# Layer 3 of a four-layer convolution network: the steps that make the next quarter's band matrices stand behind every second turn of patch products, four or five at a time

## The chip, the core and the metric

The kernel runs on one core of one Trainium2 chip, as one program. The metric is the device time of an execution in microseconds; the time before is the median of three runs.

## The reference

The input `x` is 16 images of 64 x 64 pixels with 256 channels, float32. Four layers follow each other, each of the form x = x + layer(groupnorm(x)): layer 0 is a linear attention over the pixels, layer 1 a channel and spatial gate with a state-space scan, layer 2 a 3 x 3 involution, layer 3 a 7 x 7 involution. Only layer 3 is touched here:

```python
r = jnp.einsum('bhwc,cd->bhwd', x, w_reduce)                 # 256 -> 64 channels
r = jax.nn.relu((r - mean) * (gamma / jnp.sqrt(var + BN_EPS)) + beta)
kgen = jnp.einsum('bhwd,de->bhwe', r, w_span) + b_span       # 49 weights for each of 16 groups
kgen = kgen.reshape(B, H, W, G, K * K)
...
out = jnp.einsum('bhwgk,bhwkgc->bhwgc', kgen, patches)       # each pixel: its own 7 x 7 kernel
```

Each pixel makes its own 7 x 7 kernel for each of 16 groups of 16 channels, and applies it to its neighbourhood.

## The kernel before

The kernel is written with a tile framework: the Python code issues instructions engine by engine, pools hand out buffers, and a scheduler decides in which order each engine's instructions stand and puts in the semaphore waits. The order in the code is the main guide of that scheduler, not the last word: it may take an instruction ahead of others of the same engine.

In layer 3 an image is cut into tiles of 3 x 8 output pixels (`TR, TC = 3, 8`): 22 rows of 8 tiles, 176 tiles, and the 16 groups into four quarters of four groups. A tile's input is a patch of 9 x 14 = 126 pixels. The products are matrix products over those 126 pixels:

- `reduced` (line 1425, tile `pr`) makes the 64 channels of `r`, and ACT writes them into `rt` (line 1432). One image has 11 such steps, issued during the image before, one every third turn (`features`); each loads a tile `c3` two turns ahead.
- `matrices(i, quarter)` is a generator of 24 steps per quarter. Each step makes the 126 x 24 band matrix columns of four output pixels for all 176 tiles: four matmuls (line 1458) write a PSUM tile `pk` of two banks, and then either four ACT activations (line 1468) or one VectorE add (line 1473) write it, with the bias, into the SBUF tile `wm`. Steps 1, 3, 6, 8 and 11 of each twelve go to ACT, the others to VectorE. [...]
- `involution7` (line 1524) is one turn of patch products: 32 matmuls, each of 126 rows by 32 columns, multiply the patches `xw` with the matrices `wm` into the PSUM tile `pa`. ACT (line 1536) and VectorE (line 1537) pick the group with a mask and write `ex`; GpSimd (line 1544) adds the residual `rx`. `pa` and `pr` share a PSUM pool `sm` of two buffers.

[...]

The main loop goes over 704 turns: 16 images, four quarters, 11 turns. SP issues all DMAs: the patches four turns ahead (two loads of 256 KB per turn, six `xw` buffers), the residual two turns ahead, the stores of `ex` three turns behind. The table `STEPS` says how many steps of the next quarter's matrices are issued behind each turn:

```python
for n, (i, quarter, t) in enumerate(turns):
    ...
    if t == 0:
        making = iter(())
        if n + NTT < len(turns):
            making = matrices(*turns[n + NTT][:2])
    ...
    involution7(i, quarter, t, wms[i, quarter], msk, pats.pop(0), ex[:, t % 2], rx[:, t % 2])
    ...
    for _ in range(STEPS[t]):
        next(making, None)
    if n in features:
        tp, k = features[n]
        reduced(k, tp, cs.pop((tp, k)))
    if t == NTT - 1:
        next(making, None)
```

The last line runs once more behind turn 10 (`NTT` is 11). With the table before, all 24 steps are issued by then, and it only ends the generator.

Of the kernel before, what the change touches and what calls it, by code (L numbers as in the profile page):

```python
# [36 lines left out]
def network(ctx: ExitStack, tc: tile.TileContext, a: dict, out: bass.AP):  # L37
# [767 lines left out]
    def centred_strips(i, u, xc, cen, mean):  # L805

        nc.gpsimd.tensor_tensor(
            cen.rearrange("p q t c -> p t q c"),
            xc.rearrange("p t (q c) -> p t q c", q=4),
            mean.rearrange("p (q c) -> p q c", q=4).unsqueeze(1).broadcast_to([P, 4, 4, 64]),  # L810
            ALU.subtract,
        )
        parts = []
        copies = [(u + 3, 0)] + [(u - 5, 1)] * (u >= TC - 3) + [(u + TC + 3, -1)] * (u < 3)
        for w, dt in copies:
            for th in range(2):
                t0, t1 = max(0, th * 4 + dt), min(NTC, th * 4 + 4 + dt)
                s0 = t0 - th * 4 - dt
                parts.append((
                    strips[i, :, 3 : 3 + HW, w, t0:t1, :].rearrange("q r t c -> r q (t c)"),  # L820
                    cen[th:P:2, :, s0 : s0 + t1 - t0, :].rearrange("p q t c -> p q (t c)"),
                ))
        return parts
# [540 lines left out]
    with ExitStack() as st:  # L1364
# [183 lines left out]


        turns = [(i, quarter, t) for i in range(NI) for quarter in range(4) for t in range(NTT)]  # L1550
        STEPS = (3, 2, 2, 3, 2, 3, 2, 2, 3, 2, 0)
        wms, cs, strip_stores = {}, {}, []
        features = {
            4 * NTT * i + 3 * k + 1: (2 * k, i + 1) for i in range(NI - 1) for k in range(NTT)
# [13 lines left out]
        for n, (i, quarter, t) in enumerate(turns):  # L1568
# [40 lines left out]
            if n % gap == 2 and n // gap < NCH:  # L1609
                cen = wk.tile([P, 4, 4, 64], F32, tag="xw", name="cen", bufs=6)  # L1610
                strip_stores.extend(centred_strips(NI - 1, n // gap, xc, cen, mean))
            for _ in range(STEPS[t]):
                next(making, None)
# [140 lines left out]
```

## Time and profile before

| | |
|---|---|
| median of 3 runs | 7944.51 us (7941.79 to 7947.63) |
| the profiled execution | 7971.0 us, span 7969.2 us |
| granted TensorE clock, mean over the span | 0.948 of full speed |
| busy share of the span | PE 86%, PEld 64%, DVE 71%, ACT 62%, POOL 38% |
| layer 3's main loop | 5682.9 to 7963.1 us of the span |
| in layer 3 (5690 to 7960 us) | PE busy 1966 us, ACT 1256, DVE 1047, POOL 452; DMA share 0.83 at 255 GB/s; clock 0.97 |

In the profile PE is TensorE's matmul, PEld its weight load, DVE VectorE, ACT ScalarE, POOL GpSimd and SP the engine that issues the DMAs. A row of the order of time has the start in us, the duration in us, the engine, the line, what is written and read, the shapes, how many instructions are merged in it, and in brackets the idle time before it and what ended it. A row of the waits has who waited for whom, the total in us, the number of times and the longest. A row of the chain has start, duration and what. A share of busy time is a mean over stages with different limits, so the stage is read by itself.

### The profile page before, as it was taken

How to read it: one execution, taken by the hardware profiler on the slowest of the kernel's cores; microseconds unless marked ns; L12 is line 12 of the kernel's file. 1: busy time of each engine (PE TensorE's matmuls, PEld its weight loads, DVE VectorE, ACT ScalarE, POOL GpSimd, SP SyncE). 2: the span in 40 equal slices, each digit the busy share in tenths (PEclk: the TensorE clock that was granted, in tenths of full speed). 3: DMA queues.
4: the chain of work that ended last, by engine and by line, in shares of the span. 5: the costliest groups of instructions: out<-in, count | busy, mean ns of one | idle time of the engine just before them, and what ended most of it. 6: DMA issues, size and time to landing. Idle time of an engine off the chain costs nothing.

```text
span 7969.2 us, 213876 instructions
## 1 busy us (share of the span) xinstructions
PE 6865.4 (86%) x88812; PEld 5137.4 (64%) x88812; DVE 5671.4 (71%) x6527; ACT 4934.1 (62%) x11456; POOL 3053.4 (38%) x2171
## 2 busy tenths in 40 slices
PE   7888888888888977689989999999788888888887
PEld 4666666666666664156666666666577777777776
DVE  6777777777777765879999999999444444444444
ACT  3555555555555554978787777776455555555554
POOL 1222222222222221168888888888222221111112
PEclk9999999999999986899999999999899999999999
DMA  7644444444443333967888888876688888888887
GB/s 216 196 149 133 138 137 133 135 135 135 134 137 112 117 103 103 327 209 264 285 282 286 270 287 275 288 265 224 209 259 260 258 255 261 256 253 258 248 257 236
DMA packets 1075308, 1689.89 MB, mean 212 GB/s; under 512 B 136273, under 2 KB 680354, under 8 KB 1073186
## 3 DMA queue, kind: packets, MB, share of 16 engines
q1 hardware_dynamic: 1074338, 1676.21, 65.4%
q8 instruction: 700, 11.47, 0.6%
q14 instruction: 270, 2.21, 0.1%
HBM read 1228.85 MB, written 469.76 MB: 213 GB/s over the span
## 4 chain that ended last, share of the span: by engine, by line
PE 46%; DVE 23%; issue 12%; ACT 8%; DMA 7%; POOL 3%; SPq 1%; DVEq 0%; POOLq 0%; ACTq 0%
PE pk L1458 13%; DVE pd L1185 9%; PE pa L1524 8%; PE pkv L270 5%; PE py L412 5%; DMA xn<-in_x 2%; PE pq L258 2%; PE pr L1425 2%; DVE x L1357 2%; PE pctx L336 2%; PE px L1097 1%; DVE mq L371 1%; ACT sq L421 1%; DVE z L1008 1%; DVE mq L378 1%
## 5 line engine op out<-in xcount | busy, mean ns | idle before, releaser
L1185 DVE TENSOR_TENSOR pd<-xs,pw 128x4608 f32<-128x4608 f32 x256 | 1256.0, 4947 | 5.5 <-POOL x L1199 5.3
L1458 PE MATMUL pk<-rt,span 64*128 64x176 f32 x12288 | 1183.6, 329 | 61.2 <-issue 55.0
L1468 ACT ACTIVATE wm<-pk,spanb 128x176 f32<-128x176 f32 x2560 | 845.8, 425 | 574.3 <-PE pk L1458 572.5
L1544 POOL TENSOR_TENSOR ex<-ex,rx 128x192 f32<-128x192 f32 (+2 forms) x768 | 436.7, 570 | 1826.5 <-DVE ex L1537 1329.4
L1198 POOL TENSOR_TENSOR pd<-pd 128x2048 f32<-128x2048 f32 (+2 forms) x384 | 1072.2, 2792 | 88.5 <-DVE pd L1185 68.4
L1458 PEld LDWEIGHTS pk<-rt,span 64*128 64x128 f32 x12288 | 973.2, 192 | 139.0 <-issue 81.3
L1537 DVE SCALAR_TENSOR_TENSOR ex<-pa,msk,ex 128x192 f32<-128x192 f32 x704 | 294.2, 418 | 1019.2 <-ACT ex L1536 951.9
L270 PE MATMUL pkv<-wq,xn 128*128 128x256 f32 x4096 | 979.3, 385 | 3.6 <-ACT va L279 2.0
L1524 PE MATMUL pa<-wm,xw 126*32 126x48 f32 x45056 | 751.1, 214 | 213.8 <-issue 201.0
L1473 DVE TENSOR_TENSOR wm<-pk,spanb 128x704 f32<-128x704 f32 x896 | 794.0, 888 | 192.0 <-PE pk L1458 188.8
L270 PEld LDWEIGHTS pkv<-wq,xn 128*128 128x128 f32 x4096 | 782.1, 194 | 229.3 <-issue 116.4
L366 POOL TENSOR_TENSOR qa<-qa,mq 128x1024 f32<-128x1024 f32 x256 | 501.5, 1980 | 1027.3 <-DVE mq L371 514.2
L1524 PEld LDWEIGHTS pa<-wm,xw 126*32 126x32 f32 x45056 | 620.8, 111 | 396.1 <-issue 352.0
L1147 PE MATMUL pt<-ident,pad 128*128 128x128 f32 x4608 | 604.6, 280 | 146.0 <-ACT xs L1151 122.7
L1147 PEld LDWEIGHTS pt<-ident,pad 128*128 128x128 f32 x4608 | 505.3, 142 | 294.1 <-ACT xs L1151 145.9
L1357 DVE TENSOR_REDUCE x<-pd 128x512 f32<-128x4608 f32 x128 | 634.0, 4953 | 4.4
L412 PE MATMUL py<-wo,o 128*128 128x256 f32 x2048 | 542.5, 422 | 64.8 <-ACT va L279 59.7
L1151 ACT COPY xs<-pt 128x512 f32<-128x512 f32 x1152 | 584.4, 597 | 17.5 <-PE pt L1147 17.4
L258 PE MATMUL pq<-xn,wq 128*128 128x512 f32 x1024 | 539.7, 644 | 34.1 <-ACT xn L133 21.6
L412 PEld LDWEIGHTS py<-wo,o 128*128 128x128 f32 x2048 | 496.2, 310 | 110.2 <-ACT va L279 76.9
L1536 ACT ACTIVATE ex<-pa,msk 128x192 f32<-128x192 f32 x704 | 299.7, 426 | 389.6 <-PE pa L1524 179.7
L1097 PE MATMUL px<-x2p,wis 128*128 128x512 f32 x1024 | 477.5, 610 | 46.1 <-ACT xs L1151 36.9
(243 smaller groups left out, 11780.3 us busy)
## 6 DMA issues: line engine op xcount, KB each, us to landing
xw<-strips SPq DMA_DIRECT2D x1408, 256.0 KB
xn<-in_x SPq DMA_DIRECT2D x256, 512.0 KB
x_d<-x SPq DMA_DIRECT2D x256, 512.0 KB
strips<-cen SPq DMA_DIRECT2D x352, 256.0 KB
xin<-in_x SPq DMA_DIRECT2D x128, 512.0 KB
x<-in_x SPq DMA_DIRECT2D x128, 512.0 KB
xm<-x_d SPq DMA_DIRECT2D x128, 512.0 KB
x2p<-x_d SPq DMA_DIRECT2D x128, 512.0 KB
```

Source lines behind the costliest of these rows:

```text
L258: nc.tensor.matmul(pq, lhsT=wq[:, h, f0 : f0 + P], rhs=xn[:, h], start=(h == 0), stop=(h == 1),)
L270: nc.tensor.matmul(pkv[:, q], lhsT=xn[:, h, q * P : (q + 1) * P], rhs=wq[:, h, f0 + P : f0 + 384], start=(h == 0), stop=(h == 1),)
L412: nc.tensor.matmul(py[:, q, :], lhsT=om[i, hf][:, :, ch * 4 + q], rhs=wo[:, hf, :], start=(hf == 0), stop=(hf == 1),)
L1147: nc.tensor.transpose(pt[:, k, h * P : (h + 1) * P], lines[:, h, rc * 4 + e + k, 2 * j : 2 * j + P], ident,)
L1151: nc.scalar.copy(xs[:, e : e + 2, j, :], pt)
L1185: nc.vector.tensor_tensor(pd.rearrange("p r (g f) k -> p r g f k", f=16), run, pw.rearrange("p r (g k) -> p r g k", k=9).unsqueeze(3).broa ...
L1198: nc.gpsimd.tensor_tensor(pd[..., 0:n], pd[..., 0:n], pd[..., n : 2 * n], ALU.add)
L1357: nc.vector.tensor_reduce(x3[:, :, P:C], pd1, AX.X, ALU.add)
L1458: nc.tensor.matmul(pkv[:, b, m], lhsT=span[half, first + gg, s0 : s0 + P], rhs=rto[half, o // 4 * 2 + m, :], start=True, stop=True,)
L1468: nc.scalar.activation(dst[:, m // 2, m % 2], pkv[:, m // 2, m % 2], AF.Identity, bias=spanb[:, g0 + m : g0 + m + 1],)
L1473: nc.vector.tensor_tensor(dst, pkv, spanb[:, g0 : g0 + 4].rearrange("p (b m) -> p b m", b=2).unsqueeze(3).broadcast_to([P, 2, 2, NTL]), AL ...
L1524: nc.tensor.matmul(pav[p0 : p0 + 32, :, tj * TC : (tj + 1) * TC].rearrange("c g (w v) -> c g w v", v=2), lhsT=xw[0:TILE_IN, k, tj, 32 * q ...
```

## The change

One line of the table changes. Counted over a quarter, 24 steps behind turns 0 to 9 become 23 behind turns 1, 3, 5, 7 and 9; the call behind turn 10 then issues the 24th.

```diff
         turns = [(i, quarter, t) for i in range(NI) for quarter in range(4) for t in range(NTT)]
-        STEPS = (3, 2, 2, 3, 2, 3, 2, 2, 3, 2, 0)
+        STEPS = (0, 5, 0, 4, 0, 5, 0, 4, 0, 5, 0)
         wms, cs, strip_stores = {}, {}, []
```

## The prediction

> **What bounds the kernel now.** I read three views of layer 3, the only stage that the diff touches (its first patch product starts at 5682.9 us and its last at 7963.1 us: 2280 us, 704 turns of 3.24 us, 64 quarters of 35.6 us). First the chain of work that ended last, in order of time, for a stretch of that stage:
>
> ```profile
> 7003.57 1.99 PE pk L1458 x24
> 7005.56 0.91 PE pa L1524 x57
> 7006.47 1.77 PE pk L1458 x16
> 7008.24 0.90 PE pa L1524 x58
> 7009.14 1.39 PE pk L1458 x16
> 7010.54 0.83 PE pr L1425 x8
> 7011.37 0.53 PE pa L1524 x30
> 7011.90 1.54 issue
> ```
>
> Everything on it is PE, or "issue": PE waited for nothing that the profile shows. ACT, VectorE, GpSimd and DMA do not appear. Over the whole stage the chain is PE and 11.4% issue, with some 6% of DMA and DMA issuing. Second, the waits of the stage:
>
> ```profile
> PE pa L1524 <- issue: 200.7, 197, 3.2
> PE pk L1458 <- issue: 55.0, 60, 2.4
> PEld pa L1524 <- DMA xw<-strips: 16.6, 46, 1.9
> PEld pa L1524 <- DVE wm L1473: 9.9, 30, 1.6
> PEld pa L1524 <- ACT wm L1468: 3.5, 15, 0.6
> ```
>
> The work that matters for this change, PE waiting until ACT or VectorE has emptied a PSUM buffer, costs some 15 us today. The idle time of "issue" is 256 us. Third, what this issue is: PE alone in order of time,
>
> ```profile
> 7013.44 0.58 PE L1524 MATMUL pa<-wm,xw 126*32 126x48 f32 x31 [1.54 <-issue]
> 7013.95 2.06 PE L1458 MATMUL pk<-rt,span 64*128 64x176 f32 x24
> 7015.94 0.96 PE L1524 MATMUL pa<-wm,xw 126*32 126x48 f32 x64
> 7016.83 1.01 PE L1458 MATMUL pk<-rt,span 64*128 64x176 f32 x9
> 7018.46 0.86 PE L1458 MATMUL pk<-rt,span 64*128 64x176 f32 x7 [0.62 <-issue]
> ```
>
> From one stall to the next PE ran 31 + 24 + 64 + 9 = 128 matmuls, each with its weight load: 256 instructions. The stall falls in the middle of runs, so it is no dependence. And the page's queue table has
>
> ```profile
> q8 instruction: 700, 11.47, 0.6%
> ```
>
> that is 700 transfers of 16.4 KB, and 2 x 88812 PE instructions with the 1622 of its sequencer make 179,246 = 700 x 256. So PE gets its program in blocks of 256 instructions and stands still when the next block is late. Counting the trace's records by blocks: 459 blocks in the stage, 4.96 us each on average; the q8 transfer for the next block starts 2.3 us (median) after a late block has begun (1.4 to 3.5), and PE goes on 2.44 us after it started. So a block hardly takes less than about 4.75 us, whatever is in it, and 280 of 458 begin late (over 0.35 us after the block before). PE's own work in a block, from the rows without stalls, is 4.1 us. The stage is bound by PE work and by instruction blocks in turn: each block costs the larger of the two.
>
> [...]
>
> **The change part by part.** It issues the same 24 steps per quarter, each of 4 matmuls in the program (8 weight loads and 8 matmul records) and one VectorE add or four ACT activations, no DMA. Before, 2 or 3 stand behind each of ten turns. After, five or four stand behind turns 1, 3, 5, 7, 9, and the 24th comes from the closing call behind turn 10. GpSimd's order is the same; on SP the same DMAs stand in a slightly different order (the loads of c3 and the stores of out shift by a turn at most), and I cost that at nothing: SP issues for 1960 of 2270 us and PE waits 25 us for xw in all; if that cover goes, the price is in the third rival.
>
> (a) Fewer changes of matmul form on PE. A run of 24 costs 1.99 us and one of 16 1.39 us, so 8 weight loads cost 0.60 us and entering a run 0.19 us; a turn's 64 products take 0.90 us up to the next run, of which 64 x 0.012 us (distance of weight loads inside the run) explains 0.77. Each avoided change there and back thus saves 0.19 + 0.13 = 0.32 us; by the distances between records (pk to pa 0.387 against 0.07 inside, pa to pk 0.185 against 0.012) it is 0.49 us. One might expect ten changes to become six per quarter, but the scheduler puts single pk matmuls ahead of or between the products: in the instruction order the returns to pa fall from 693 to 547. 146 x 0.32 to 0.49 = 47 to 72 us; I take -60, between the two rows.
>
> (b) New waits for PSUM buffers. pk has three buffers. With runs of 2 or 3 steps the fourth step never stands close behind the first. Now it does. From the ACT and VectorE rows: four activations take 1.33 us, an add 0.89 us, and the addition of the last turn's ex (0.42 us each on ACT and VectorE) stands ahead. Counting from the start of the run (pk at 7003.50, its first add 7004.41, its first activations 7005.07): the add of step 1 ends at 1.8 us, the activations of step 2 at 2.9 us; without a wait steps 4 and 5 would start at 1.8 and 2.4 us. Which steps ACT empties is fixed (1, 3, 6, 8, 11 of each 12). Run by run: in [add act add act add] the fifth step waits 0.5 us for step 2's activations; [add act add act] waits for nothing; in [add add act add act] the fifth waits 0.2 us for the second add; [add act add add] waits for nothing; in [act add act add add] the fourth waits 0.44 us for the activations of the first (0.9 to 2.24 us after the start). Together 1.14 us per quarter, 63 quarters: 72 us. The 24th step is emptied by ACT and stands right ahead of the next quarter's first turn, whose second product reads it: 0.2 us to the first activation and 1.33 us for the four, less 0.55 us of pk matmuls that the order slips in: 1.0 to 1.5 us, 63 to 95 us in all. Sum 135 to 167 us; bounds 0 (a wait cannot be negative; all of it may fall in time in which PE would wait for instructions) and 200 (the split runs delay further steps); I take 150. Behind such a wait on PE stand the products of the next turns and, every third turn, the matmuls of pr; ACT's and VectorE's ex, GpSimd's addition and the stores wait in turn, all with room (ACT is busy 1256 of 2270 us, VectorE 1047, GpSimd 452).
>
> (c) 138 more waiting instructions in PE's stream (685 for 547 in the stage), 0.05 us each by their rows: 7 us.
>
> Raw sum on PE: -60 + 150 + 7 = +97 us, between -65 and +160.
>
> (d) The blocks. Two turns of products back to back are 256 instructions, one block, in 1.8 us of PE work. I laid both orders out in blocks of 256, added up the durations above in each, and took 4.75 us wherever a block has less. Without any waits of (b): before 2232 us (measured 2280; the rest is chiefly what PE waited for DMA), after 2249: +17 although PE's work fell by 64, since blocks with under 2.5 us of work go from 5 to 55. With waits where they fall: blocks above 4.75 us go from 80 to 141, and the sum rises by 69 us; with 4.5 us for 4.75 it is 82, with 5.1 us 54. So the shortest block time hides about a third of (b). A further part goes because PE asks for the next block earlier when it has instructions in hand: blocks that had 0.7 to 1.2 us to spare asked 1.4 us after their start, not 2.3. I subtract a fifth for that: **+55 us**.
>
> The profiled execution took 7971.0 us (span 7969.2), 26.5 us over the median of 7944.5. So I expect a profile of about 8026 us and a median of 7944.5 + 55, about 8000 us.
>
> **Rivals.** Slower by far more: 55 blocks are used up in 2 us, the pair of turns needs two xw tiles at once, and SP (86% busy) has no room to catch up. The wait for xw then joins the sum: +69, and about 1 us per quarter, 64 us: about +135, 8080 us. For it: xw waits exist already. Against it: loads run four turns ahead, 13 us. It decides once the waits for xw, 25 us now, pass 90.
>
> No change: block loading alone sets the pace, 460 blocks for 459, the waits of (b) fall wholly inside late blocks. 0 to +15 us, 7945 to 7960. For it: 61% of the blocks begin late. Against: every full block takes part of the waits on its own.
>
> Faster: (a) reaches the end. Place: PE between turns. That needs the emptying to keep pace (waits under 60 us) and a shortest block time near 4 us: a burst holds PE for 3 us with only 80 instructions, in which the block for the next pair might come in time. With 4.0 us and no waits the tally gives -6, with no shortest time -64; I price it at -35, 7910 us. Against it: the 0.44 and 0.5 us come from plain durations, and the transfers show hardly a block under 4.2 us after a late one.
>
> **How the numbers follow.** My forecast (+16 to +95 us) 0.58; far slower 0.12; no change 0.14; faster 0.16. Differences under 0.2%, 16 us, cannot be told from none by measuring this kernel. So slower 0.70, same 0.14, faster 0.16. The range runs from 7925 (it takes in no change and the near half of faster) to 8070 (raw sum with all waits on the path, +125).
>
> **What would show it.** Right: in the profile after, "PE pk <- ACT wm" and "PE pk <- DVE wm" appear, together some 100 us, "PE pa <- ACT wm" some 60 about once per quarter; issue on PE stays above 200 us and moves from the middle of products after one turn to pairs of turns; runs of pa come as 128. (a) is wrong if the distances at changes of form do not cost 0.3 to 0.5 us any more. (d) is wrong if blocks with two turns last well under 4.2 us. The whole is wrong if the waits for wm stay below 50 us or the waits for xw pass 90.

## The result, and the profile after

The changed kernel takes 8000.2 us (median of 6 runs, 7979.7 to 8017.2), the kernel before on the same chip 7946.1 us (6 runs, 7937.2 to 7972.1). The ratio is 1.0065, with a 95% interval from 1.0044 to 1.0086: slower by 54 us on the medians, where +55 was predicted. Run again later it was 1.0064 (experiment 7). The profiled execution took 7992.8 us (span 7991.0), 22 us more than that of before and not 55: that of before was 26.5 us above the median then shown, this one is 7.5 us below its own.

The queue table still has the same number of instruction transfers:

```profile
q8 instruction: 700, 11.47, 0.6%
```

So PE has as many blocks to load as before; the 138 waiting instructions more (684 for 546 in the stage) are about half a block. Next come the waits of layer 3 in the changed kernel (who waited for whom, us in total, times, longest):

```profile
PE pa L1524 <- issue: 165.5, 138, 3.6
PE pk L1458 <- issue: 88.3, 63, 2.8
PEld pk L1458 <- ACT wm L1468: 52.4, 116, 0.6
PEld pa L1524 <- ACT wm L1468: 25.7, 95, 1.0
PEld pk L1458 <- DVE wm L1473: 25.7, 88, 1.0
PEld pa L1524 <- ACT rt L1432: 17.0, 54, 0.4
PEld pk L1458 <- ACT ex L1536: 13.5, 46, 0.3
PEld pa L1524 <- DVE ex L1537: 12.6, 57, 0.4
PEld pa L1524 <- DMA xw<-strips: 4.6, 19, 1.0
```

Two rows are as before in sum: issue on PE is 253.8 us (before 255.7), in fewer and longer stalls, 201 for 257. The next six say that PE's weight loads now wait for ACT and VectorE. They come to 147 us, where such rows made 23 before (9.9 and 3.5 for wm, 3.4, 3.3 and 3.1 for ex and rt). The last says that the patches arrive in good time: the rival in which they do not is gone.

PE alone in order of time shows where a stall of issue now falls:

```profile
7028.19 1.76 PE L1458 MATMUL pk<-rt,span 64*128 64x176 f32 x20 [0.69 <-issue]
7030.17 1.46 PE L1458 MATMUL pk<-rt,span 64*128 64x176 f32 x16 [0.22 <-ACT wm L1468]
...
7045.06 0.70 PE L1524 MATMUL pa<-wm,xw 126*32 126x48 f32 x41 [1.30 <-issue]
7045.69 2.71 PE L1458 MATMUL pk<-rt,span 64*128 64x176 f32 x30
7048.34 0.90 PE L1524 MATMUL pa<-wm,xw 126*32 126x48 f32 x57
7049.86 1.09 PE L1524 MATMUL pa<-wm,xw 126*32 126x48 f32 x71 [0.63 <-issue]
```

The last four rows are the same arithmetic as in the prediction: 41 + 30 + 57 = 128 matmuls between two stalls, 256 instructions with their weight loads. (Each matmul of the program leaves two such records and two weight loads: the page of before has 12288 of each at line 1458, for 6144 in the program.) The places of the stalls bear the blocks out: from the start of one weight load or waiting instruction of PE to the next more than 0.8 us pass 219 times in the stage of before, 203 of them at the same two neighbouring places of a count of PE's instructions by 256, and 167 times in the changed kernel, 165 of them there. The first two rows are a burst of five steps, less its first four matmuls, which stand ahead of the stall; behind step three it stops for 0.22 us for an emptied PSUM buffer. The chain of waits cannot be set beside that of before: followed back from the end, it breaks off at 7964.3 us, ahead of which it has nothing.

So I read the stage from the records in another way. From each weight load of PE to the next I took the distance that is usual for that pair of tiles (pk to pk 0.0685 us, pa to pa 0.0115, pk to pa 0.386, pa to pk 0.183, from the kernel before). These usual distances are the first two columns: between two loads of the same tile (inside runs), and where the tile and so the form of the matmul changes (form changes). What a distance has above that is put down to a late block (above 0.15 us, at a multiple of 256 instructions), to half clock (a granted clock of 0.5, with any wait that falls into it), to a wait (above 0.12 us elsewhere), or to the rest. All in us, from the stage's first product to its last, one execution each:

| kernel | stage | inside runs | form changes | late blocks | waits | half clock | rest |
|---|---|---|---|---|---|---|---|
| before | 2280 | 1377 | 468 | 341 | 28 | 75 | -9 |
| changed | 2309 | 1389 | 385 | 321 | 156 | 68 | -11 |
| changed, run again | 2336 | 1389 | 385 | 343 | 153 | 77 | -11 |
| 24th step alone late | 2285 | 1372 | 501 | 318 | 38 | 68 | -12 |
| 24th step early | 2318 | 1395 | 344 | 325 | 212 | 60 | -18 |
| changed, split emptying | 2276 | 1393 | 362 | 263 | 213 | 47 | -2 |
| before, two tiles | 2265 | 1380 | 450 | 349 | 22 | 69 | -4 |
| changed, two tiles | 2288 | 1392 | 368 | 357 | 60 | 84 | +28 |
| steps in threes, two tiles | 2353 | 1408 | 260 | 432 | 81 | 121 | +51 |

The two executions of the changed kernel agree within 3 us in the columns of work and of waits; the 27 us between them lie in late blocks and half clock. So a difference of some 20 us in one of these two columns is not read as an effect, and each of the other kernels has one execution only.

### The profile page after: what moved, and what is told of

It is laid out like the page before. It is cut to its first block, busy times and chain, and to the rows that moved or that the text cites. A ratio compares the mean times of both kernels' runs of the same rounds, so it can differ in the third digit from the quotient of the medians.

```text
span 7991.0 us, 213998 instructions
## 1 busy us (share of the span) xinstructions
PE 6890.5 (86%) x88812; PEld 5156.3 (65%) x88812; DVE 5681.8 (71%) x6527; ACT 4935.8 (62%) x11456; POOL 3050.5 (38%) x2171
## 5 line engine op out<-in xcount | busy, mean ns | idle before, releaser
L1458 PE MATMUL pk<-rt,span 64*128 64x176 f32 x12288 | 1234.7, 336 | 117.8 <-issue 88.3
L1458 PEld LDWEIGHTS pk<-rt,span 64*128 64x128 f32 x12288 | 1008.6, 196 | 253.9 <-issue 112.5
L1524 PE MATMUL pa<-wm,xw 126*32 126x48 f32 x45056 | 714.9, 213 | 178.8 <-issue 165.5
```

What stands on the lines that cost most here:

```text
L1458: nc.tensor.matmul(pkv[:, b, m], lhsT=span[half, first + gg, s0 : s0 + P], rhs=rto[half, o // 4 * 2 + m, :], start=True, stop=True,)
L1524: nc.tensor.matmul(pav[p0 : p0 + 32, :, tj * TC : (tj + 1) * TC].rearrange("c g (w v) -> c g w v", v=2), lhsT=xw[0:TILE_IN, k, tj, 32 * q ...
```

## The experiments

All times are set against the kernel before on the same chip in the same session. Theory A says that waits for PSUM buffers make the change slower, partly hidden behind late instruction blocks; theory B says that the uneven blocks alone, or mainly, do.

**1. The 24th step alone, in the kernel before.** Its last step moves from turn 8 to the closing call, as in the change.

```diff
-        STEPS = (3, 2, 2, 3, 2, 3, 2, 2, 3, 2, 0)
+        STEPS = (3, 2, 2, 3, 2, 3, 2, 2, 2, 2, 0)
```

> The kernel before with one step less behind turn 8, so that the 24th step comes from the closing call behind turn 10, as in the change; nothing else is bunched. Theory A (PE waits until ACT and VectorE have emptied PSUM buffers, part of it hidden behind late instruction blocks): the first turn of each quarter waits 1.0 to 1.5 us for the four activations of that step, 63 times; PE pa <- ACT wm rises from 3.5 to 60 to 90 us in the stage and the time by 20 to 50 us over the kernel before. Theory B (only the uneven instruction blocks cost: two turns of products back to back use up a block in 2 us): the blocks are those of before, 0 +- 8 us.

Measured: ratio 1.0008 (0.9998 to 1.0017), medians 7976.3 and 7969.1 us. The row that theory A rested on:

```profile
PEld pa L1524 <- ACT wm L1468: 20.2, 50, 1.0
```

20 us for 3.5 before, not 63 to 95. It costs 7 us by the medians and 14 at most by the interval, which can't be told from nothing: inside theory B's 0 +- 8 us and outside theory A's 20 to 50. The 24th step was much oversized in the prediction: the row has 50 waits in 63 quarters, 0.4 us on average, where 1.0 to 1.5 us was worked out.

**2. The changed kernel with the 24th step in its bursts.**

```diff
-        STEPS = (0, 5, 0, 4, 0, 5, 0, 4, 0, 5, 0)
+        STEPS = (0, 5, 0, 5, 0, 5, 0, 4, 0, 5, 0)
```

> The changed kernel with five steps instead of four behind turn 3, so that all 24 steps are issued by turn 9 and the closing call issues none. Theory A: the waits at the quarter's start go (PE pa <- ACT wm under 8 us), those inside the bursts stay or grow by 0.4 us per quarter: 15 to 40 us under the changed kernel, 10 to 40 us over the kernel before. Theory B: the blocks are as uneven as in the change: within 8 us of the changed kernel, 50 us over the kernel before.

Measured: ratio 1.0044 (1.0032 to 1.0056).

```profile
PEld pk L1458 <- ACT wm L1468: 99.4, 242, 1.1
PEld pa L1524 <- ACT wm L1468: 4.1, 17, 0.6
```

The wait ahead of the quarter's first turn went (25.7 to 4.1 us), and the one inside the bursts doubled (52.4 to 99.4). Form changes fell by another 41 us and waits rose by 56 in the ledger. The time is 33 us over the kernel before, which theory A had (10 to 40) and B had not (50); it is some 16 us under the change (1.0064, experiment 7), give or take 16. So the kernel that waits more is not the slower one. A step that leaves one place of the stage waits in another.

**3. The emptying of a step split between ACT and VectorE.** Each step's four activations or one add become two activations and an add of half the size, so that a buffer might come free sooner. It was run with the change and, as control, without.

```diff
-                    if (q * 12 + n) % 12 in (1, 3, 6, 8, 11):
-                        for m in range(4):
...
+                    for m in range(2):
+                        nc.scalar.activation(
+                            dst[:, 0, m], pkv[:, 0, m], AF.Identity,
+                            bias=spanb[:, g0 + m : g0 + m + 1],
+                        )
+                    nc.vector.tensor_tensor(
+                        dst[:, 1], pkv[:, 1],
...
```

> The changed kernel, with each step emptied by both engines: two activations on ACT (about 0.7 us) and an add of half the size on VectorE (about 0.5 us) instead of four activations (1.33 us) or one add (0.89 us) by turns. Theory A: no wait inside a burst is left (PE pk <- ACT wm and <- DVE wm together under 15 us), the one at the quarter's start is half as long: 40 to 70 us under the changed kernel, -15 to +15 us against the kernel before. Theory B: as the changed kernel, +50 us, since the blocks are the same.

> The kernel before with the same emptying by both engines: the control of the run on the changed kernel. Theories A and B: PE waits 15 us for these buffers in the whole stage today, so at most 15 us less, and more VectorE instructions that are off the path: -15 to +8 us against the kernel before.

Measured: with the change 1.0024 (1.0013 to 1.0035), without 0.9980 (0.9972 to 0.9989). What was meant to remove the waits did not, as the group of the add and a row of the waits of the changed kernel with split emptying show:

```profile
L1471 DVE TENSOR_TENSOR wm<-pk,spanb 128x352 f32<-128x352 f32 x1511 | 794.2, 526 | 644.8 <-ACT wm L1467 588.3 <-PE pk L1458 3.1 <-issue 0.5
```

```profile
PEld pk L1458 <- DVE wm L1471: 143.5, 331, 2.1
```

The add was ordered behind the step's own activations: VectorE waited 588 us for ACT, and PE 143.5 us for VectorE. Both read one PSUM tile; with a tile for each, in experiment 4, the add waits for PE alone, 230.9 us with the change. The miss shows something else. In the ledger waits rose from 156 to 213 us against the change, and late blocks fell from 321 to 263. That looks like a trade of the one for the other, as theory A has it, but it is not shown as a rule: in experiment 2 waits rose as much (212) and late blocks stayed (325). And with these longer waits the change's penalty fell, from 0.64% to 0.44% (1.0024 over 0.9980), 33 us by the medians.

**4. Two PSUM tiles of half the size.** As 3, but each step writes two tiles, so ACT and VectorE empty them side by side.

```diff
-                    pk = wg.tile([P, 2, CT], F32, tag="wg", name="pk")
-                    pkv = pk[:, :, 0 : 2 * NTL].rearrange("p b (m t) -> p b m t", m=2)
+                    pkv = [
+                        wg.tile([P, CT], F32, tag=f"wg{b}", name=f"pk{b}")[
+                            :, 0 : 2 * NTL
+                        ].rearrange("p (m t) -> p m t", m=2)
+                        for b in range(2)
+                    ]
```

> The changed kernel, each step emptied by both engines at once: the PSUM tile pk becomes two tiles of one bank, two activations on ACT empty the one, an add of half the size on VectorE the other (in the earlier run with one tile the add still stood behind the activations, 1.3 us one after the other). Theory A (PSUM waits): PE waits for wm under 30 us in the stage, and the time is within 15 us of the control (the same emptying in the kernel before). Theory B (uneven instruction blocks): the waits go all the same, but 25 to 45 us over the control remain, since two turns of products still use up a block in 2 us.

> The kernel before with the two tiles and the emptying by both engines: the control. Theories A and B: 10 to 25 us less than the kernel before, as the control with one tile showed 16 us less.

Measured: with the change 1.0019 (1.0009 to 1.0028), without 0.9978 (0.9968 to 0.9988). The waits of the changed kernel with two tiles:

```profile
PE pa L1524 <- issue: 176.1, 160, 4.3
PE pk L1462 <- issue: 101.6, 73, 3.2
PEld pa L1524 <- DMA xw<-strips: 20.3, 50, 3.2
PE pr L1425 <- DMA c<-c_d: 17.4, 8, 4.6
PEld pa L1524 <- ACT wm L1471: 13.0, 58, 0.4
PEld pk L1462 <- DVE wm L1475: 1.9, 2, 1.0
```

Now the bursts hardly wait for the emptying: 103.8 us in the three rows of wm became some 16. The change's penalty goes from 0.64% to 0.41% (1.0019 over 0.9978), a fall of 0.23%, about 18 us, with an uncertainty of some 15 us from the four intervals. And 0.41%, 33 us (27 by the medians), stays without these waits, inside theory B's 25 to 45 us and outside theory A's 15. That the 18 us are what the waits cost is not shown: with the split emptying of experiment 3 the penalty fell as far, to 0.44%, while the waits grew. What the two pairs share is that each step is emptied by both engines; what of it brings the fall, no run separates. So the waits cost some 18 us of the whole, give or take 15, if all of the fall is theirs, and perhaps nothing: far less than their rows add up to. In the ledger, from changed (mean of two executions, 2322 us) to changed with two tiles (2288), waits fall by 95 us, while late blocks rise by 25 and the rest by 39, and 15 of the 34 us that remain are what two tiles also bring to the kernel before; 34 us is little more than lies between two executions. Some of the time saved goes to DMA: the waits for xw and c, 4.6 and 1.3 us in the changed kernel, are 20.3 and 17.4 us here.

Two tiles without the change beat both: 7956.1 us against 7971.0, 0.22% less. The split emptying of one tile did as well without the change (0.20% less).

**5. Shorter matmuls in the steps.** The matmuls of a step run over 88 of the 176 tiles, and the emptying copies the 88 columns twice: half of the band matrices' columns are left out. PE has less work per block, so if the shortest block time sets the pace, less is gained than the work that is taken away.

```diff
-                                rhs=rto[half, o // 4 * 2 + m, :],
+                                rhs=rto[half, o // 4 * 2 + m, 0 : NTL // 2],
```

> The kernel before with the steps' matmuls over 88 of the 176 tiles; the emptying engines copy the 88 columns twice (VectorE in two adds), so the second half of the matrices is a copy of the first. PE gets exactly the same number of instructions, but each weight load and matmul of a step takes nearly half as long, 0.03 to 0.04 us less for 12288 of them: 370 to 490 us less PE work in the stage. If instruction blocks set a shortest time of about 4.75 us for 256 instructions (theories A and B both use this), the stage cannot go below 459 x 4.75 = 2180 us: 50 to 120 us less than the kernel before. If the idle time of issue were something else, the time would fall by 250 us or more.

> The changed kernel with the same shortened matmuls. Theory A: bursts now wait at every step for the emptying engines (0.9 us per step for 0.35 us of PE), but nearly all blocks are shorter than the shortest time, so most of it is hidden: 0 to 40 us over the shortened kernel before. Theory B: nearly every block is at the shortest time in both, so the unevenness no longer matters: -10 to +10 us.

Measured: 1.0390 (1.0369 to 1.0411) without the change and 1.0481 (1.0464 to 1.0499) with it: slower by 3.9% for less work, where 50 to 120 us less was expected. It can't decide between the theories, since the clock changed. The stretches from 5690 to 6500 us, first of the kernel before, then of the kernel before with short matmuls (stretch, its length, busy time and instructions of PE, PEld, DVE, ACT and POOL, granted clock, DMA share, GB/s):

```profile
5690.00:6500.00 810.00, 701.72 (x20526) 594.12 (x20524) 369.86 (x579) 447.79 (x1325) 164.96 (x272) 0.96 0.84 259
```

```profile
5690.00:6500.00 810.00, 673.27 (x18232) 584.23 (x18232) 346.86 (x790) 398.30 (x1175) 145.91 (x241) 0.79 0.75 227
```

PE ran fewer matmuls in the same time, at a granted clock of 0.79 for 0.96. The time in which the stage ran at half clock went from 126 to 1147 us. Why is open; the last section has what the records show.

**6. Half as many instructions for the products.** The matmuls of a turn go over 96 columns and not 48, on every second patch only, so that a turn has 64 PE instructions for 128: odd tiles use their neighbour's patch, which leaves half of the patches out of the products. All else, the patches' loads among it, stays; two PSUM tiles are used as in 4. If blocks set the pace, the control must become much faster, and the change's penalty must go or turn round.

```diff
-            for tj in range(NTC):
+            for tj in range(0, NTC, 2):
...
-                            pav[p0 : p0 + 32, :, tj * TC : (tj + 1) * TC].rearrange(
-                                "c g (w v) -> c g w v", v=2
+                            pav[p0 : p0 + 32, :, tj * TC : (tj + 2) * TC].rearrange(
+                                "c g (w v) -> c g w v", v=4
```

> The control with two PSUM tiles (steps 2 or 3 behind each turn), with half as many patch products of twice the width: each matmul takes the matrices of two neighbouring tiles (96 columns instead of 48) with the patch of the first, so odd tiles get their neighbour's patch. PE streams the same columns with 64 instead of 128 instructions per turn; the stage has some 280 instruction blocks instead of 459, each with about 6.5 us of work. If instruction blocks are what issue stands for (theories A and B): nearly no block is late, the idle time of issue falls from 250 to under 40 us and the time by 200 to 330 us against the kernel before. If not, the time stays within 60 us of the control.

> The same halving in the changed kernel with two PSUM tiles. Theory B (the remaining 30 us of the change come from blocks made uneven): with no block short of work the sign turns: only the saved changes of matmul form are left, 20 to 60 us less than the halved control. Theory A (what remains are PSUM waits and other waits on PE): still 15 to 40 us more than the halved control.

Measured: 0.9832 (0.9818 to 0.9847) without the change, 0.9830 (0.9810 to 0.9850) with it. The queue table and two waits of the control:

```profile
q8 instruction: 523, 8.57, 0.5%
```

```profile
PE pa L1524 <- DMA xw<-strips: 147.4, 236, 3.2
PE pr L1425 <- DMA c<-c_d: 73.0, 39, 6.9
```

Issue, 253.5 us of the matmuls' waits at pa and pk in the control of 4, is no longer among them; on the weight loads of pa 105.8 us are left, in 440 gaps of 0.24 us. Counted by blocks, 7 of 282 begin more than 0.35 us late, 9.5 us in all, at 7.6 us per block, where the control of 4 has 282 of 460 with 353 us, at 4.93. That settles what "issue" is: the same columns in fewer instructions hardly have it, so it goes with the number of instructions. The time fell by only 135 us, where 200 to 330 was expected, because the DMA of the patches became the next bound: the chain of this kernel has 28% of DMA for xw, where that of the control of 4 has 1.1%.

The penalty of the change is gone (7833.4 and 7833.6 us), although the change in the order of the steps is the same. This fits blocks as its cause, but in a stage that the patches now bound any small cost of PE could be hidden too, so it doesn't separate the theories by itself.

**7. Steps in threes, and the change again.** Eight steps stand behind turns 2, 5 and 8, with two PSUM tiles: fewer changes of form still, and blocks more uneven still. In the same way the changed kernel ran once more.

```diff
-        STEPS = (3, 2, 2, 3, 2, 3, 2, 2, 3, 2, 0)
+        STEPS = (0, 0, 8, 0, 0, 8, 0, 0, 8, 0, 0)
```

> The control with two PSUM tiles with the steps behind every third turn, eight at a time, STEPS (0, 0, 8, 0, 0, 8, 0, 0, 8, 0, 0): three turns of products stand back to back, 384 instructions in 2.5 us. Theory B: blocks with under 2.5 us of work go from 10 to 99, and the sum of the larger of work and 4.75 us rises by 80 us over the control, where the change raises it by 7: 60 to 120 us over the control, against 28 for the change. Theory A: the emptying by both engines keeps up (0.72 us on ACT for 0.60 us of PE), about 0.6 us per burst and 192 bursts, while more changes of form are saved: within 40 us of the control.

> The changed kernel unchanged, timed again for a narrower interval beside the same kernel before as the runs with two PSUM tiles. Those runs put what is left of the change without PSUM waits at 0.41% (1.0019 against 0.9978). If the PSUM waits carry the rest of the first result, this ratio lies at 1.0055 to 1.0075, and the waits are worth 0.15 to 0.35%; if they cost nothing in the end (all hidden behind late instruction blocks), it lies at 1.0035 to 1.0045.

Measured: threes 1.0084 (1.0064 to 1.0104), the change 1.0064 (1.0048 to 1.0080), which agrees with the first result. It lies where the expectation put it if the waits for PSUM buffers carry the rest; but by the split pair of experiment 3 (0.44% with longer waits) that does not follow from it. Over the control of 4 (0.9978, each against the kernel before in its own session) threes are slower by 1.06%, 84 us, inside B's 60 to 120 and outside A's 40. PE in order of time, steps in threes:

```profile
6805.17 1.36 PE L1524 MATMUL pa<-wm,xw 126*32 126x48 f32 x90 [0.18 <-ACT rt L1432]
6807.85 0.67 PE L1524 MATMUL pa<-wm,xw 126*32 126x48 f32 x38 [1.32 <-issue]
6808.45 0.90 PE L1425 MATMUL pr<-c,wr 128*64 128x192 f32 x8
6809.28 0.56 PE L1462 MATMUL pk<-rt,span 64*128 64x176 f32 x2
6809.77 1.15 PE L1524 MATMUL pa<-wm,xw 126*32 126x48 f32 x79
6812.09 0.78 PE L1524 MATMUL pa<-wm,xw 126*32 126x48 f32 x49 [1.17 <-issue]
6812.80 5.04 PE L1462 MATMUL pk<-rt,span 64*128 64x176 f32 x62
```

Three turns of products in a row stall once or twice (38 + 8 + 2 + 79 = 127 matmuls and one record missing), and the eight steps behind them take 5.04 us with only 128 instructions (64 matmuls, of which two stand ahead). In the ledger the form changes cost 190 us less than in the control, and yet the stage is 88 us longer: late blocks +83, waits +59, half clock +52, rest +55, inside runs +28. Blocks shorter than 4.2 us go from 77 to 115, and the mean block from 4.93 to 5.12 us. Fewer changes of form did not pay here, where the instructions come in bunches.

## Why the prediction was right, step by step

- **What bounds the stage: right.** PE and instruction blocks in turn. Taking instructions away (experiment 6) took the idle time of late blocks away, 353 to 9.5 us; bunching them (experiment 7) lengthened it, 349 to 432 us in the ledger.
- **(a) Fewer changes of form, -60: right.** The ledger has -83 at the changes and +12 inside the longer runs, about -70, at unchanged distances. Late blocks hardly moved (-20 and +2 us in the two executions), so they did not take the saving back; the new waits, +128 in the ledger, are more than it. With two tiles, where the PSUM waits are nearly gone, the same -70 is there and the stage is still 23 us longer.
- **(b) New waits, +150 on PE: right in size, wrong in part.** The rows give 147 - 23 = 124 us. Inside the bursts 78 us stand where 72 was worked out. Ahead of the quarter's first turn there are 26, not 63 to 95: experiment 1 has that alone, 20 us. Not foreseen were the 43 us of the last three rows of ACT and VectorE above (`rt` and `ex`), two of which fall on the products (`rt` 17.0 and `ex` 12.6, before 2.5 and 3.1): two turns and a `pr` now follow each other closely, and share the two buffers of `sm`.
- **(c) 138 more waiting instructions, +7:** too small to be told from the rest column, which did not move (-9 and -11).
- **Not foreseen: less waiting for DMA.** PE's waits for xw fell from 16.6 to 4.6 us, and those of `pr` for c from 27.8 to under 2. I had priced the DMAs at nothing or as a loss. With two tiles most of both is back.
- **(d) What the blocks hide: the sum is right, partly by luck.** The tally had 17 us without any waits and 52 more with them, both less a fifth: some 14 and 41. The runs show 33 (27 by the medians) without the waits for wm, and for these waits some 18 if all of the fall is theirs, perhaps nothing. So the uneven blocks, with whatever else comes with the bunches, cost about twice what I gave them, and the waits less than half. The two errors nearly cancel in +55, and that they do is luck.
- **What was behind the tally of (d).** Thin blocks did cost: counted from the weight loads, blocks with under 2.5 us of work at the usual distances go from 10 to 52 (I had 5 to 55), and the idle time in them from 28 to 120 us (127 in the second execution; with two tiles from 41 to 123). But 4.75 us is no shortest time. It is the sum of two medians: 198 of the 459 blocks of the kernel before took less, and the thin blocks after the change last 4.3 us on average (4.5 in the second execution), 21 and 18 of the 52 under the 4.2 us that I had named as the sign. Which term of the tally made up for that is not shown. In the changed kernel with two tiles, 70 us of work less came back as waits (+38), half clock (+15), late blocks (+8) and small delays (+32).
- **The rivals.** "Far slower" needed the waits for xw above 90 us: 4.6. "Faster" needed waits under 60 us, and even where they were (two tiles) the change stayed slower by 0.41%. "No change" was right in that most of the waits' time does not show in the kernel's, and wrong in that the bunching costs something itself. (700 x 256 is 179,200, and not 179,246 as I wrote; the blocks don't depend on it.)

What stays open is how the 33 us divide: the ledger spreads them over four columns, two of which vary by about as much from one execution to the next; and what the waits for PSUM buffers cost in the end, between nothing and some 18 us.

## What to carry to other kernels

If PE's idle time is called issue and falls every 128 matmul records, look whether loading the program is the bound. Here fewer instructions took that idle time away (353 us of late blocks to 9.5), and bunching like work, which saves changes of matmul form (83 us), made more blocks of 256 short instructions that were not loaded in time (10 to 52 blocks with under 2.5 us of work, their idle time 28 to 120 us). Here the bunches also asked for more PSUM buffers at once (147 us of such waits for 23). In this stage, bound by two things in turn, 103.8 us of waits cost some 18 us, or nothing that shows; so price a wait by taking it away in both kernels, not by adding the row up, and look at a pair in which it grows as well.

## What the hardware showed that I had not expected

- The granted clock in the records is 1 or 0.5, the latter in pieces of 3.41 us or a multiple (before: 27 single, 3 double and 1 triple piece between 5690 and 7950 us, 123 us). Long idle times of PE do not account for them: in the kernel with short matmuls PE is idle for more than 3.41 us four times there, as often as before, and it has 99 pieces of half clock, 939 us. No run here shows what lowers the clock.
- PE, busy for 1966 of 2270 us in the stage of before, still lost 256 us to the loading of its own program: 77% of its instructions there are the small products and their weight loads, and 256 of these alone take 1.75 us (the 128 products of two turns after the change), far less than the 4.75 us or so (2.3 + 2.44, medians) in which the next block comes.
- Two engines that empty parts of one PSUM tile were put behind each other by the scheduler; with a tile for each they ran side by side (VectorE's wait for ACT, 588 us with the split tile, is no longer among the waits of its add). The kernel before became 0.22% faster with that, but 0.20% faster with one split tile too, so running side by side is not shown to be what helped.
